# Two weight blocks loaded one step earlier, and two tiles of attention swapped, in a one-core masked attention kernel

## The chip, the cores and the metric

The kernel runs on one core of a Trainium2 chip. The metric is the device time of one execution in microseconds (us). The core's engines are TensorE (PE, with its weight loads as PEld), VectorE (DVE), ScalarE (ACT), GpSimd (POOL) and SyncE (SP). SP, ACT and POOL also issue transfers (DMAs), which run on the core's 16 DMA engines.

## The reference, cut to what matters

```python
h = jnp.maximum(_layernorm(x, axis=-1), 0.0)        # x: 2708 x 1024, float32
q = h @ W_q.T + b_q ; k = h @ W_k.T + b_k ; v = h @ W_v.T + b_v
z = (q @ k.T) / sqrt(1024)
z = z * adj ; z = jnp.where(z == 0.0, -10000.0, z)  # adj: 2708 x 2708 of 0 and 1, some 4 ones in a row
out = x + relu(softmax(z, axis=1) @ v)
```

`adj` is sparse, so a row of the attention has a handful of neighbours, and all other scores carry no weight. A row with no neighbour gets the mean over all rows.

## The kernel before, in words

**What is multiplied.** The kernel folds W_q and W_k into one matrix M, so that "q" means h @ M, and a score is the product of a q row with a neighbour's h row. W_v is applied behind attention, to the weighted sum of h rows. So there are two dense products, h @ M for the queries and u @ W_v for the outputs. Rows are sorted by their number of neighbours and cut into 21 tiles of 128 rows and a rest; tile t has K[t] slots for neighbours (tile 17 three, tile 13 five).

**Units.** Tiles go through TensorE in pairs ("units"): ten q pairs (units 0 to 9; the last, `last_q` = 9, holds tiles 18 and 19), then ten o pairs, (6, 5), (4, 3) and so on along the list `order`, and then the lone tile 8 (`alone`; its transposed rows are `T_alone`). A pair is multiplied by a seven-product scheme on 2 x 2 blocks. The blocks of the weight stand in `M[:, i, j]`, and combinations of them in `T[:, 0..3]`, which lies in the buffer `wlow`. The operands of a unit's own rows are `a11`, `a12`, `a22` and the sums `s1` to `s4`. One product is four matmuls of 128x512, eight records in the profile.

**The order of one unit.** `multiply(n)` makes five products, calls `between(n)`, which opens the next unit with its first two products (`opened(n + 1)`: a11 x M[0,0], and then s1 x T[:,0] for a q pair, s1 x M[0,1] for an o pair), and makes unit n's own last product, a22 x T[:,3]. Between the products `after(i)` puts in everything else: attention steps, loads of coming rows, and near the end of the q pairs the exchange of M for W_v.

**The exchange.** With B the blocks of W_v: B12 (less B11) goes to M[0,1] two units ahead. B22 is loaded into T[:,0], B11 into M[0,0], both at `after(0)` of the last q pair, and B21 into M[1,0] at its `after(3)`. VectorE then makes T[:,1], T[:,2] and T[:,3] from them by subtraction (the lines `nc.vector.tensor_sub(place, a, b)`), and ScalarE copies B22 on to M[1,1]. Two buffers in T[:,0] then serve attention's gathers. In the profile these loads are `wlow<-in_wv_dram` and `M<-in_wv_dram`.

**Attention** is a stream of VectorE steps that is fed into the units in portions (`advance`). For a tile: `fetch` loads its q rows (`pq`; from `q_late`, where the q pairs store them, for tiles from 8 on) and asks for the h rows of its neighbours (`g`, gathered by POOL into buffers as these come free); `scores` multiplies (line 863); `weights` forms the softmax; `sums` adds up u (line 923). u goes to `u_dram`, and the o pair's rows (`or`) come back from there.

**What sets the order.** In this part of the program VectorE keeps the order in which the code is written. The order on the other engines and queues is set by a scheduler ahead of time. Each engine and each queue works through its list in order.

Of the kernel before, what the change touches and what calls it, by code (L numbers as in the profile page):

```python
# [65 lines left out]
def tile_preln_masked_attention(  # L66
# [12 lines left out]
    nc = tc.nc  # L79
# [120 lines left out]
    M = core.tile([P, 2, 2, 4, NB], FT, name="M")  # L200
# [108 lines left out]
    def follow(steps):  # L309

        for step in steps.split():
            first, *only = step[1:].split(".")
            first, *last = first.split("-")
            first = int(first or 0)
            if step[0] == "s":
                stats(range(first, int(last[0] if last else first) + 1))
            elif step[0] == "m":
                moments(first)
            elif step[0] == "r":
                root(first)  # L320
            elif step[0] == "a":
                apply(first, *[range(int(o[0]), int(o[-1]) + 1) for o in only])
            elif step[0] in "hk":
                keep(first, step[0] == "h")
            elif step[0] == "+":
                owe(first)
            elif step[0] == "p":
                counted(first)
            elif step[0] == "c":
                counts(*halves[first])  # L330
            elif step[0] == "o":
                sorted_at.append(sort(*halves[first]))
            elif step[0] == "w":
                pooled.close()
                with tc.issue_after((behind if first < EARLY else products)[-1].ins):
                    entered.append(put(first, int(last[0]) + 1))
            elif step == "z":
                pooled.enter_context(tc.manual_schedule(engines={mybir.EngineType.Pool}))
                with tc.issue_after(entered[-1].ins):
                    reload(EARLY, NT)  # L340
            elif step[0] == "b":
                reload(*halves[first])
            elif step[0] == "g":
                squared(first)
            else:
                if step[0] == "e":
                    counted(first)
                if step[0] != "j":
                    found(first, *[range(int(o[0]), int(o[-1]) + 1) for o in only])
                if step[0] != "i":  # L350
                    listed(first)
# [81 lines left out]
    T = wlow.rearrange("p (k a) (b w) -> p k (a b) w", a=2, b=2)  # L433
# [12 lines left out]
    with tc.tile_pool(name="w", bufs=1, side="left") as wp:  # L446
# [11 lines left out]
        t1 = [work.tile([P, D], FT, tag="hT", name=f"t1_{k}", bufs=2) for k in range(2)]  # L458
# [145 lines left out]
    def small(name):  # L604
        return half.tile([P, NB], FT, tag="half", name=name, bufs=14)
# [380 lines left out]
    done, held, ws, us = set(), {}, {}, {}  # L986
    formed = set()
    faced_tiles, whole_second = set(), []
    order = [6, 5, 4, 3, 2, 0, 20, 7, 17, 13, 18, 12, 19, 11, 15, 10, 14, 1, 16, 9, 8]
    assert sorted(order) == list(range(FULL))  # L990
    chain = placed
    stream = attention(order[:order.index(0)] + [SECOND] + order[order.index(0):])
# [15 lines left out]
    def add_block(bank, a, b, last=True):  # L1008
        for c in range(4):
            mm = nc.tensor.matmul(bank, a[:, c, :], b[:, c, :], start=False, stop=(c == 3), skip_group_check=True)  # L1010
        return mm
# [3 lines left out]
    def opened(n):  # L1015

        if n not in banks_of:
            return
        X, Z = banks_of[n]
        ops = ops_of[n][0]  # L1020
        add_block(X, ops["a11"], M[:, 0, 0])
        Y = psum.tile([P, NB], FT, tag="acc", name="psy")
        nc.scalar.copy(Y, X)
        if n == FIRST:
            follow("o0")
        products.append(add_block(Z, ops["s1"], T[:, 0] if units[n][0] == "q" else M[:, 0, 1]))
        p5 = small("p5")
        nc.scalar.copy(p5, Z)
        opened_of[n] = Y, p5

    def between(n):

        if n == len(units) - 1:
            single["first"] = one_started(single["banks"], single["turned"][:, 0:4, :])
        else:
            opened(n + 1)

    def one_started(banks, a):

        X, Z = banks  # L1040
        add_block(X, a, M[:, 0, 0])
        first = small("p_single")
        nc.scalar.copy(first, X)
        return first

    def multiply(n, results, after):


        X, Z = banks_of.pop(n)
        ops = ops_of.pop(n)[0]  # L1050
        Y, p5 = opened_of.pop(n)
        after(0)
        after(1)
        products.append(add_block(Y, ops["s2"], T[:, 1]))
        u2 = small("u2")
        nc.scalar.copy(u2, Y)
        after(2)
        add_block(X, ops["a12"], M[:, 1, 0])
        results[0](X)
        after(3)  # L1060
        products.append(add_block(Z, ops["s4"], M[:, 1, 1]))
        results[2](Z, u2)
        after(4)
        products.append(add_block(Y, ops["s3"], T[:, 2]))
        results[1](Y, p5)
        after(5)
        between(n)
        add_block(Y, ops["a22"], T[:, 3])
        results[3](Y)
        after(6)  # L1070
# [119 lines left out]
    def of_wv(i, j):  # L1190

        return wv[j][:, i * 4:(i + 1) * 4, :]
# [26 lines left out]
    last_q = len(q_pairs) - 1  # L1219
# [13 lines left out]
    for n, unit in enumerate(units):  # L1233
# [15 lines left out]
        def after(i):  # L1249
# [15 lines left out]
                    with tc.issue_after(sorted_at[-1].ins):  # L1265
                        nc.vector.memset(g, 0.0)
            b11, t1, b21, b22 = M[:, 0, 0], M[:, 0, 1], M[:, 1, 0], M[:, 1, 1]
            for at, place, src in (((-2, 0), t1, of_wv(0, 0)), ((0, 0), T[:, 0], of_wv(1, 1)), ((0, 0), b11, of_wv(0, 0)),
                                   ((0, 3), b21, of_wv(1, 0))):
                if (n - last_q, i) == at:  # L1270
                    nc.sync.dma_start(place, src)
            if (n - last_q, i) == (0, 4):
# [302 lines left out]
```

## Time and profile before

| | us |
|---|---|
| median of 3 timed runs | 630.40 |
| lowest and highest | 630.32, 631.99 |
| the profiled execution | 635.63 |
| its span, first to last instruction | 633.9 |
| TensorE busy | 623.0 (98%) |
| VectorE busy | 525.2 (83%) |
| GpSimd busy | 370.7 (58%) |
| ScalarE busy | 291.6 (46%) |

All times inside the profile count from the span's start. A row of a timeline reads: start, duration, engine, line, operation, output<-inputs, count; in brackets the idle time of that engine ahead of it and what ended it. The mean granted clock of TensorE over the span is 0.994 of full speed.

### The profile page before, as it was taken

To read this page: it belongs to the slowest core of one execution; us is meant where nothing else is said; L and a number is where in the kernel's file an instruction comes from. 1 tells how busy PE (TensorE), PEld (TensorE's weight loads), DVE (VectorE), ACT (ScalarE), POOL (GpSimd) and SP (SyncE) were. 2 spreads that over 40 slices of the span, in tenths; PEclk is the share of its full clock that TensorE was granted. 3 is DMA by queue.
4 is the path that set the end of the run, shared out by engine and by line. 5 is a ranking of instruction groups with operands and counts; after the bars stand their busy time and mean duration, and the time that the engine had idled before them with its cause. 6 is when DMAs were issued, how large, how long until landed. Compare 5 with 4: busy or idle time off the path is not lost.

```text
span 633.9 us, 6066 instructions
## 1 busy us (share of the span) xinstructions
PE 623.0 (98%) x1579; PEld 312.0 (49%) x1579; DVE 525.2 (83%) x1022; ACT 291.6 (46%) x421; POOL 370.7 (58%) x394
## 2 busy tenths in 40 slices
PE   9999999999998999999999989999999999999996
PEld 5777766444444544444444434444444444444442
DVE  5999879898897845899897879998988998988741
ACT  3538985749477372443332333444433324342300
POOL 2639960885766677666543432878566776762241
PEclk9999999999999999999999989999999999999999
DMA  8999997598788469996686999899999999996391
GB/s 333 407 365 316 340 351 301 207 320 307 262 257 337 135 196 369 296 410 191 207 343 197 362 346 305 261 335 318 330 285 344 291 297 307 341 286 172 102 295 71
DMA packets 65089, 182.19 MB, mean 287 GB/s; under 512 B 9960, under 2 KB 20024, under 8 KB 64409
## 3 DMA queue, kind: packets, MB, share of 16 engines
q0 software_dynamic: 26656, 86.02, 43.3%
q1 hardware_dynamic: 31594, 71.53, 32.7%
q10 hardware_dynamic: 6798, 24.20, 9.8%
q8 instruction: 14, 0.23, 0.2%
q14 instruction: 27, 0.21, 0.1%
HBM read 146.70 MB, written 43.36 MB: 300 GB/s over the span
## 4 chain that ended last, share of the span: by engine, by line
PE 96%; DMA 3%; issue 0%; POOL 0%; SPq 0%; DVE 0%; ACT 0%; POOLq 0%
PE ps L1010 44%; PE psy L1010 32%; PE ps_y L476 6%; PE ps_x L476 4%; PE ps_z L476 4%; PE pt L415 3%; DMA M<-in_wv_dram 2%; DMA qr<-h_dram,tab 1%; PE ps_y L511 1%; PE ps_h L1226 0%; PE ps_v L594 0%; DVE y_alone L1391 0%; POOL out_dram L1375 0%; ACT q L1101 0%; POOLq L1397 0%
## 5 line engine op out<-in xcount | busy, mean ns | idle before, releaser
L610 POOL DMA_INDIRECT g<-h_dram,tab x93 | 120.5, 1296 | 62.7 <-ACT u L912 21.7
L1010 PE MATMUL ps<-M,a 128*128 128x512 f32 x320 | 145.8, 599 | 2.0 <-DMA M<-in_wv_dram 2.0
L1010 PE MATMUL psy<-wlow,s 128*128 128x512 f32 x320 | 145.1, 596 | 0.0
L863 DVE SCALAR_TENSOR_TENSOR junk<-g,pq 128x1024 uint8<-128x1024 f32 x92 | 112.4, 1221 | 11.8 <-issue 4.9
L1010 PE MATMUL ps<-M,s 128*128 128x512 f32 x240 | 107.9, 592 | 0.0
L1010 PEld LDWEIGHTS ps<-M,a 128*128 128x128 f32 x320 | 60.4, 192 | 75.4 <-issue 71.2
L1010 PEld LDWEIGHTS psy<-wlow,s 128*128 128x128 f32 x320 | 60.6, 192 | 72.9 <-issue 71.9
L923 DVE SCALAR_TENSOR_TENSOR u<-g,coef,u 128x1024 f32<-128x1024 f32 x70 | 89.7, 1281 | 5.5 <-ACT u L912 4.0
L389 DVE FIND_INDEX8 at<-ones,adj 128x8 uint32<-128x685 f32 (+1 forms) x88 | 74.5, 865 | 0.0
L1010 PEld LDWEIGHTS ps<-M,s 128*128 128x128 f32 x240 | 45.5, 190 | 57.2 <-issue 56.5
L1010 PE MATMUL psy<-wlow,a 128*128 128x512 f32 x160 | 71.9, 592 | 0.0
L368 ACT ACTIVATE sized<-adj 128x2708 uint8<-128x2708 f32 (+1 forms) x22 | 54.2, 2465 | 7.9 <-DMA adj<-in_adj_dram 6.6
L1111 POOL DMA_INDIRECT y<-in_x_dram,tab x19 | 34.6, 1821 | 35.6 <-ACT y L1128 24.2
L298 POOL TENSOR_TENSOR hsum<-hsum,x 128x256 f32<-128x256 f32 (+1 forms) x56 | 38.8, 738 | 25.5 <-DVE wlow L444 21.4
L1010 PEld LDWEIGHTS psy<-wlow,a 128*128 128x128 f32 x160 | 30.4, 190 | 38.3 <-issue 37.1
L808 POOL DMA_INDIRECT out_dram<-y,tab x21 | 27.0, 1287 | 19.2 <-issue 13.1
L1010 PE MATMUL ps<-wlow,s 128*128 128x512 f32 x80 | 36.0, 593 | 0.0
L944 ACT COPY v<-u 128x1024 f32<-128x1024 f32 x19 | 19.8, 1044 | 29.1 <-DVE u L923 25.8
L760 ACT COPY ps<-bp_sb 128x512 f32<-128x512 f32 x42 | 24.6, 595 | 10.3 <-DVE y L1146 9.7
L626 POOL DMA_INDIRECT tab_dram<-tab,pos_i x22 | 21.7, 985 | 11.2 <-DVE pos_i L689 5.7
L276 ACT ACTIVATE x<-x,r 128x1024 f32<-128x1024 f32 (+1 forms) x22 | 25.8, 1232 | 5.2 <-POOL r L266 5.2
L912 ACT ACTIVATE u<-g,coef 128x1024 f32<-128x1024 f32 x16 | 18.4, 1149 | 21.3 <-DVE coef L911 13.2
(253 smaller groups left out, 843.4 us busy)
## 6 DMA issues: line engine op xcount, KB each, us to landing
adj<-in_adj_dram SPq DMA_DIRECT2D x21, 1354.0 KB
x<-in_x_dram SPq DMA_DIRECT2D x21, 512.0 KB
h_dram<-x ACTq DMA_DIRECT2D x21, 512.0 KB
u_dram<-v ACTq DMA_DIRECT2D x19, 512.0 KB
or<-u_dram SPq DMA_DIRECT2D x76, 128.0 KB
q_late<-q SPq DMA_DIRECT2D x12, 512.0 KB
pq<-q_late POOLq DMA_DIRECT2D x12, 512.0 KB
M<-in_wv_dram SPq DMA_DIRECT2D x3, 1024.0 KB
```

Source lines behind the costliest of these rows:

```text
L276: nc.scalar.activation(xs[i][:n], xs[i][:n], AF.Relu, bias=r[:n, 4, i:i + 1], scale=r[:n, 3, i:i + 1])
L298: small.append(nc.gpsimd.tensor_add(hsum[:n, cols], hsum[:n, cols], xt[:n, cols]))
L368: nc.scalar.activation(sized[:n], a[:n, :, :PW], AF.Abs, accum_out=total[:n, t:t + 1])
L389: nc.vector.max_index(at[:n, k - first_k, g, :], ones[:n, 0:8], a[:n, g, :])
L476: mm = nc.tensor.matmul(bank, a_tile(o + H * a[0], a[1], i), b(o), start=first and o == 0, stop=(o == H - 1), skip_group_check=True)
L610: return nc.gpsimd.indirect_dma_start(out=dst, out_offset=None, in_=src, in_offset=off, bounds_check=N - 1, oob_is_err=False)
L760: nc.scalar.copy(return_[h], row[:, h * NB:(h + 1) * NB])
L808: to = nc.gpsimd.indirect_dma_start(out=out, out_offset=bass.IndirectOffsetOnAxis(ap=ptab.bitcast(U32)[:n, t, SLOTS:SLOTS + 1], axis=0), i ...
L863: chained(lambda: nc.vector.scalar_tensor_tensor(junk, g_of[t][s], 1.0, tq[t], op0=ALU.mult, op1=ALU.mult, accum_out=zall[:, t, s:s + 1]))
L923: chained(lambda: nc.vector.scalar_tensor_tensor(u, g_of[t][s], coef[:, s:s + 1], u, op0=ALU.mult, op1=ALU.add))
L1010: mm = nc.tensor.matmul(bank, a[:, c, :], b[:, c, :], start=False, stop=(c == 3), skip_group_check=True)
L1111: return nc.gpsimd.indirect_dma_start(out=y[:n], out_offset=None, in_=x, in_offset=off, compute_op=ALU.add)
```

## The change

It issues the loads of B22 and B11 directly behind the two products that open the last q pair, in `between` of the unit before, instead of at `after(0)` of the last q pair. And it swaps tiles 17 and 13 in `order`, so that attention takes 13 first; the o pair of the two is (13, 17) then.

```diff
-    order = [6, 5, 4, 3, 2, 0, 20, 7, 17, 13, 18, 12, 19, 11, 15, 10, 14, 1, 16, 9, 8]
+    order = [6, 5, 4, 3, 2, 0, 20, 7, 13, 17, 18, 12, 19, 11, 15, 10, 14, 1, 16, 9, 8]
...
         else:
             opened(n + 1)
+        if n == last_q - 1:
+            nc.sync.dma_start(T[:, 0], of_wv(1, 1))
+            nc.sync.dma_start(M[:, 0, 0], of_wv(0, 0))
...
-            for at, place, src in (((-2, 0), t1, of_wv(0, 0)), ((0, 0), T[:, 0], of_wv(1, 1)), ((0, 0), b11, of_wv(0, 0)),
-                                   ((0, 3), b21, of_wv(1, 0))):
+            for at, place, src in (((-2, 0), t1, of_wv(0, 0)), ((0, 3), b21, of_wv(1, 0))):
                 if (n - last_q, i) == at:
                     nc.sync.dma_start(place, src)
```

SyncE's queue around the loads, before and then now. `q_late<-q_2152` and `q_late<-q_2153` are the stores of q tiles 16 and 17 (the unit before the last q pair), and `or` are rows of o pairs.

```order
L1086 DMA q_late<-q_2152 128x1024
L700 DMA or_2258<-u_dram 32x4x256 x4
L700 DMA or_2263<-u_dram 32x4x256 x4
L1086 DMA q_late<-q_2153 128x1024
L1271 DMA wlow<-in_wv_dram 128x2048
L1271 DMA M<-in_wv_dram 128x2048 x2
L700 DMA or_2370<-u_dram 32x4x256 x4
```

```order
L1089 DMA q_late<-q_2152 128x1024
L700 DMA or_2258<-u_dram 32x4x256 x4
L700 DMA or_2263<-u_dram 32x4x256 x4
L1038 DMA wlow<-in_wv_dram 128x2048
L1039 DMA M<-in_wv_dram 128x2048
L1089 DMA q_late<-q_2153 128x1024
L1273 DMA M<-in_wv_dram 128x2048
```

The loads of B22 and B11 moved ahead of the store of q tile 17; the load of B21 stays behind it.

POOL's queue in the same stretch, before and then now, where `pq` is a load of a tile's q rows and `g` a gather of one neighbour slot. Before, `pq_2353` belongs to tile 17 and `pq_2434` to tile 13; now `pq_2353` belongs to tile 13 and `pq_2447` to tile 17.

```order
L845 DMA g_1428<-v_dram 64x1024
L610 DMA g_1430<-h_dram,tab 128x1024
L610 DMA g_1431<-h_dram,tab 128x1024
L610 DMA g_1432<-h_dram,tab 128x1024
L610 DMA g_1433<-h_dram,tab 128x1024
L610 DMA g_1434<-h_dram,tab 128x1024
L610 DMA g_1435<-h_dram,tab 128x1024
L610 DMA g_1425<-h_dram,tab 128x1024
L610 DMA g_1426<-h_dram,tab 128x1024
L610 DMA g_1428<-h_dram,tab 128x1024
L833 DMA pq_2353<-q_late 128x1024
L833 DMA pq_2434<-q_late 128x1024
```

```order
L845 DMA g_1428<-v_dram 64x1024
L833 DMA pq_2353<-q_late 128x1024
L610 DMA g_1430<-h_dram,tab 128x1024
L610 DMA g_1431<-h_dram,tab 128x1024
L610 DMA g_1432<-h_dram,tab 128x1024
L610 DMA g_1433<-h_dram,tab 128x1024
L610 DMA g_1434<-h_dram,tab 128x1024
L610 DMA g_1435<-h_dram,tab 128x1024
L610 DMA g_1425<-h_dram,tab 128x1024
L610 DMA g_1426<-h_dram,tab 128x1024
L610 DMA g_1428<-h_dram,tab 128x1024
L833 DMA pq_2447<-q_late 128x1024
```

The first load of q rows moved from behind the nine gathers to ahead of them; the second stays behind them.

## The prediction

> **What bounds the kernel now.** I read the page's busy times first, then its chain, then the chain in order of time, and last the instructions of each engine around the one place where the chain leaves TensorE near the edit.
>
> ```profile
> PE 623.0 (98%) x1579; PEld 312.0 (49%) x1579; DVE 525.2 (83%) x1022; ACT 291.6 (46%) x421; POOL 370.7 (58%) x394
> PE 96%; DMA 3%; issue 0%; POOL 0%; SPq 0%; DVE 0%; ACT 0%; POOLq 0%
> 197.56 5.28 DMA qr<-h_dram,tab
> 352.95 13.84 DMA M<-in_wv_dram
> 366.93 8.80 PE ps L1010 x16
> ```
>
> TensorE is busy 98% of the span and is 96% of the chain. So time can be won only where TensorE stands still or runs slowly. The chain leaves it for a transfer at two places: at 197.56 (a gather of rows for a q pair, which the change does not touch) and at 352.95, the load into M that the change issues earlier. Here is TensorE at both:
>
> ```profile
> 197.30 3.60 PE L1010 MATMUL ps<-M,s 128*128 128x512 f32 x8
> 202.98 1.54 PE L415 MATMUL pt<-ident,qr 128*128 128x128 f32 x8 [2.08 <-DMA qr<-h_dram,tab]
> 204.32 4.85 PE L1010 MATMUL psy<-wlow,s 128*128 128x512 f32 x8
> ...
> 344.13 3.60 PE L1010 MATMUL ps<-wlow,s 128*128 128x512 f32 x8
> 361.30 3.60 PE L1010 MATMUL psy<-wlow,s 128*128 128x512 f32 x8
> 366.93 5.37 PE L1010 MATMUL ps<-M,a 128*128 128x512 f32 x8 [2.03 <-DMA M<-in_wv_dram]
> 372.13 3.60 PE L1010 MATMUL ps<-M,s 128*128 128x512 f32 x8
> 375.57 3.60 PE L1010 MATMUL psy<-wlow,a 128*128 128x512 f32 x8
> ...
> 366.90:370.70 3.80, 3.77 (x5) 1.64 (x6) 1.36 (x2) 0.00 (x0) 2.86 (x3) 0.55 1.00 365
> ```
>
> One product is eight matmul records. Two products in a row start 375.57 - 372.13 = 3.44 us apart. The product at 361.30 (the last q pair) should be followed at 364.74 by the first product of the first output pair, which reads B11 from M[0,0]. It starts at 366.93: 2.19 us late. It then takes 372.13 - 366.93 = 5.20 us instead of 3.44, another 1.76 us. The window row (busy times of five engines, then the granted clock, the DMA share and GB/s) gives the reason: a clock of 0.55 in these 3.8 us. The same pair, an idle time of 2.08 us and a product of 4.85 us instead of 3.60, stands at 202.98. **What the wait for B11 costs in this execution is 2.19 + 1.76 = 3.95 us.**
>
> **The change, part by part.** *The two loads issue earlier.* SyncE's queue before:
>
> ```profile
> 338.67 4.46 SPq L700 DMA_DIRECT2D or<-u_dram  x8
> 351.81 0.34 SPq L1086 DMA_DIRECT2D q_late<-q  x1
> 352.25 0.38 SPq L1271 DMA_DIRECT2D wlow<-in_wv_dram  x1
> 352.95 5.44 SPq L1271 DMA_DIRECT2D M<-in_wv_dram  x2
> 358.49 16.24 SPq L700 DMA_DIRECT2D or<-u_dram  x8
> ```
>
> B22 (into T[:,0], "wlow") goes out at 352.25 and B11 at 352.95, because both stand behind the store of q tile 17 at 351.81, which waits for its eviction. Behind the edit they stand ahead of that store, and what they wait for is the last reader of their places: a11 x M[0,0], and then s1 x T[:,0], the product at 344.13, which ends at 347.73. So B22 can issue at about 347.8 and B11 0.7 us later, at 348.5, which is 4.45 us earlier. SyncE issued nothing between 343.1 and 351.8, so the wait at the head of its queue delays nothing there. The loads themselves cost no engine time; the count of loads stays the same.
>
> When does B11 land? The chain gives 13.84 us from issue to landing. With that, 348.5 + 13.84 = 362.3, which is 2.4 us before the 364.74 at which TensorE wants it. That it need not take longer, although nine gathers are in flight then, I bound by the traffic:
>
> ```profile
> 343.00:347.70 4.70, 4.70 (x13) 2.07 (x12) 4.59 (x5) 0.57 (x1) 3.79 (x4) 1.00 0.86 197
> 347.70:352.20 4.50, 4.50 (x12) 1.96 (x11) 4.43 (x5) 1.55 (x3) 3.55 (x4) 1.00 0.90 292
> 352.20:355.00 2.80, 2.80 (x8) 1.28 (x7) 2.80 (x5) 1.25 (x2) 2.00 (x2) 1.00 0.85 256
> 355.00:359.00 4.00, 4.00 (x11) 1.76 (x10) 3.40 (x14) 2.73 (x6) 0.73 (x1) 1.00 1.02 419
> ```
>
> From 355 on, the engines moved 419 GB/s; from 347.7 to 355 they moved 292 and 256. If the loads get nothing but that gap, they move (419 - 292) x 4.5 + (419 - 256) x 2.8 = 1.0 MB of their 2.1 MB by 355, half of what before began only then and ended at 366.8. The other half takes about half of those 11.8 us: 361. So both workings put B11 at 361 to 362.5, and the wait goes. Lower end, if they were alone at 419 GB/s: 5 us, about 353. Upper end: a duration over 16.2 us, which keeps a part of the wait.
>
> *The store of q tile 17* now stands behind 2.1 MB in the same queue. Its reader is the load of that tile's q rows ("pq"), on POOL's queue:
>
> ```profile
> 341.85 1.96 POOL L610 DMA_INDIRECT g<-h_dram,tab  x1 [7.75 <-ACT u L912]
> 353.99 1.74 POOL L610 DMA_INDIRECT g<-h_dram,tab  x1 [0.53 <-DVE u L929]
> 359.75 1.15 POOL L833 DMA_DIRECT2D pq<-q_late  x2 [4.02 <-DMA q_late<-q]
> 367.23 1.35 POOL L610 DMA_INDIRECT wlow<-h_dram,tab  x1 [6.33 <-DVE wlow L1282]
> ...
> 338.07 1.22 DVE L863 SCALAR_TENSOR_TENSOR junk<-g,pq 128x1024 uint8<-128x1024 f32 x1
> 364.17 2.29 DVE L1282 TENSOR_TENSOR wlow<-wlow,M 128x2048 f32<-128x2048 f32 x1 [1.71 <-DMA wlow<-in_wv_dram]
> 371.21 1.23 DVE L863 SCALAR_TENSOR_TENSOR junk<-g,pq 128x1024 uint8<-128x1024 f32 x1 [2.95 <-DMA pq<-q_late]
> 399.27 1.24 DVE L863 SCALAR_TENSOR_TENSOR junk<-g,pq 128x1024 uint8<-128x1024 f32 x1
> ```
>
> The store can start moving only when B11 has landed, so it lands at about 362 to 364, and POOL issues pq of tile 17 then, 2 to 4 us later than 359.75. Queued behind it on POOL are gathers into the two buffers made from T, which waited until 367.23 for VectorE's subtraction anyway, and which VectorE first uses at 399.27. Cost: nothing, with some 30 us of cover.
>
> *Tile 13 ahead of tile 17.* Its q rows were stored long before, and its pq buffer is free once the score at 338.07 is done. POOL was idle until 341.85, so this pq issues at about 339.4 and delays no gather. VectorE's wait of 2.95 us at 371.21 for tile 17's pq goes. So does its wait of 1.71 us for B22. That brings VectorE forward by 4.66 us, more than TensorE's 3.95. Both tiles keep their three and five gathers, and the gathers for both are issued by 354. No arithmetic is added.
>
> *Does the gain reach the end?* VectorE must keep up with a TensorE that is 3.95 us earlier, and the last tile must be ready:
>
> ```profile
> DVE p L1123 <- ACT taken L1077: 3.9, 4, 1.6
> DVE u L1127 <- PE ps L1010: 3.6, 5, 1.2
> 534.58 0.69 DVE L1127 TENSOR_TENSOR u<-ps,u 128x512 f32<-128x512 f32 x1 [0.57 <-PE ps L1010]
> ...
> 607.35 3.60 PE L1010 MATMUL psy<-wlow,s 128*128 128x512 f32 x8
> 609.07 1.25 DVE L705 STREAM_TRANSPOSE T_alone<-or 128x1024 f32<-128x1024 f32 x1 [10.76 <-DMA or<-u_dram]
> 610.78 3.60 PE L1010 MATMUL ps<-M,T_alone 128*128 128x512 f32 x8
> ```
>
> The two rows of waits are of the time behind 368: VectorE there stands 7.5 us in all for products and their evictions, the last such time at 534.58. So it is led by TensorE up to there and moves with it. The lone tile's transpose ends at 610.32, and its first product starts at 610.78, when 607.35 + 3.43 lets it: TensorE did not wait, but the spare time is only 0.46 us. As the work ahead of that transpose follows TensorE until 534.58, I let it move along. The cost is nothing, or some tenths.
>
> **Sum.** Against the profiled execution's own 635.63 us (span 633.9): 635.63 - 3.95 = 631.7. The median of the timed runs is 630.40, 5.2 us under the profiled one, and even under its span. TensorE runs at its full pace in the profile, so the timed runs must stand still less, or end sooner. Two losses of clock, 1.76 us here and about as much at 202.98, would be 3.5 of these 5.2 us, and the runs (630.32 to 631.99) differ by 1.67, about one such loss. So the gain in a timed run lies between 2.19 us (idle time alone) and 3.95 (with the slow product). The profile has the slow product behind both waits, the gap speaks for its absence; I take the middle, 3.1 us: 630.4 - 3.1 = **627.3 us**.
>
> On this the Trainium skill ("TensorE: Matmul & The Clock Gate", Part 1) says that the clock is halved after an idle window of about 3.4 us that runs freely, and takes a busy one to come back. The trace agrees with the length of the slow time but not with the idle time, which was 2.03 us here; by that rule alone the wait would cost its 2.19 us and the time would be 628.2. The skill's "Runtime: NRT & Kernel Launch" puts a fixed gap of about 6.2 us between a profile's total and the reported time. By that the timed runs hold the whole 3.95 us and the time would be 626.4; no run shown here can tell.
>
> **The rivals.** *B11 still late.* The loads share the queues with nine gathers; if they need over 16.2 us, a wait stays, and with it perhaps the slow clock. For it: 0.90 share of DMA at 347.7. Against: 292 GB/s there, where 419 were possible. Time: 629 to 630.4. *The gain is given back at the end.* The lone tile has 0.46 us to spare; if attention moves along only in part, TensorE waits 1 to 3 us ahead of that product instead: 629.5 to 631.5. Against: the row at 534.58. *Slower: the last tile comes later than now.* Attention's fetches are reordered for all later tiles, through buffers that come free in another order. On the old time axis the lone tile is wanted at 610.78 - 3.95 = 606.8. If its transpose ended at 610.9, 0.6 us later than now, TensorE would wait 4.1 us there and, with a slow product behind it (1.76), lose 5.9 us for the 3.95 won: 632.3 or more. That is the point from which it decides. Against: VectorE's 7.5 us of waiting behind 368 absorb that much delay. *Nothing to win in timed runs:* their loads are faster than the profiled one's, and the wait is 1 us or less: 629.5 to 630.4.
>
> **How the numbers follow.** The wait goes and the time follows: 0.62, with 625.8 to 628.5. Wait gone but under 1 us in timed runs: 0.12. B11 still late: 0.08. Given back at the end: 0.08. Slower: 0.10. About 0.3%, 1.9 us, is what a measurement of this kernel can tell from no change. So faster 0.62, within 0.28, slower 0.10. The range reaches from 625.8 (the full 3.95 and some tenths) to 630.6 (no gain), and leaves the slower case out.
>
> **What would show it.** In the changed profile: B22 and B11 issued at about 348; no idle time of TensorE for M near 365 and a clock of 1.0 there; products 3.44 us apart from 197 us' wait to the end; no wait for pq near 367 on VectorE; the store of tile 17 landing at 362 to 364; T_alone at 605 to 606. The prediction is wrong if TensorE stands still elsewhere for as long, above all ahead of T_alone, or if the timed runs had no such wait.

## The result: 627.9 us, 0.5% faster

| | before | changed |
|---|---|---|
| median of 5 timed runs, us | 631.17 | 627.91 |
| lowest and highest, us | 630.32, 631.99 | 627.52, 628.29 |
| the profiled execution, us | 635.63 | 628.18 |
| its span, us | 633.9 | 626.5 |

The ratio is 0.9953, with a 95% interval of 0.9942 to 0.9965; by the medians that is 3.26 us. (The ratios are those of fast runs as the record gives them, and can differ a little from the quotient of two medians.) The prediction was 627.3 us. The profiled execution of the changed kernel is one of its five timed runs; that of the kernel before is not among its five.

The page of the changed kernel, busy times and then the shares of the chain:

```profile
PE 619.6 (99%) x1579; PEld 310.9 (50%) x1579; DVE 525.1 (84%) x1022; ACT 291.1 (46%) x421; POOL 366.2 (58%) x394
PE 99%; POOL 0%; DVE 0%; POOLq 0%; issue 0%
```

The chain now never leaves TensorE for a transfer. Both transfers are gone from it, the load of B11 and also the gather near 197 that the change does not touch. TensorE at both places (start, duration, engine, line, what):

```profile
201.13 1.04 PE L415 MATMUL pt<-ident,qr 128*128 128x128 f32 x8
357.73 3.60 PE L1010 MATMUL psy<-wlow,s 128*128 128x512 f32 x8
361.16 3.60 PE L1010 MATMUL ps<-M,a 128*128 128x512 f32 x8
364.60 3.60 PE L1010 MATMUL ps<-M,s 128*128 128x512 f32 x8
```

The first product with B11 follows at 357.73 + 3.43 = 361.16, without idle time, and lasts 3.60 us instead of 5.37. Times here stand some 3.6 us ahead of those of before, because the wait near 197 did not happen in this execution. The queues and VectorE around the loads:

```profile
344.19 0.35 SPq L1038 DMA_DIRECT2D wlow<-in_wv_dram  x1
344.59 0.43 SPq L1039 DMA_DIRECT2D M<-in_wv_dram  x1
348.24 0.33 SPq L1089 DMA_DIRECT2D q_late<-q  x1
...
359.88 0.57 POOL L833 DMA_DIRECT2D pq<-q_late  x1 [7.74 <-DMA q_late<-q]
...
362.80 1.22 DVE L863 SCALAR_TENSOR_TENSOR junk<-g,pq 128x1024 uint8<-128x1024 f32 x1
```

The loads go out 4.05 and 3.65 us ahead of the store of q tile 17. That store lands when POOL issues the load behind it, at 359.88. VectorE's next scores, at 362.80, are those of tile 13 and wait for nothing. The traffic in the second and third of the four windows that the prediction showed, moved by the 3.6 us to the axis of this execution:

```profile
344.10:348.60 4.50, 4.50 (x12) 1.99 (x11) 4.43 (x5) 1.52 (x3) 3.57 (x4) 1.00 1.01 386
348.60:351.40 2.80, 2.80 (x8) 1.25 (x7) 2.80 (x5) 1.28 (x2) 1.98 (x2) 1.00 1.01 408
```

The loads filled most of the gap: 386 and 408 GB/s, where before there were 292 and 256. No row prints when B11 landed, but the trace holds the completion events of its load, and the last of them stands at 356.79. That is 12.2 us behind the issue and 4.4 us before TensorE wants B11.

### The profile page after: what moved, and what is told of

Same layout as the page of the kernel before. It is cut to its first block, busy times and chain, and to the rows that moved or that the text cites. A ratio compares the mean times of both kernels' runs of the same rounds, so it can differ in the third digit from the quotient of the medians.

```text
span 626.5 us, 6070 instructions
## 1 busy us (share of the span) xinstructions
PE 619.6 (99%) x1579; PEld 310.9 (50%) x1579; DVE 525.1 (84%) x1022; ACT 291.1 (46%) x421; POOL 366.2 (58%) x394
## 4 chain that ended last, share of the span: by engine, by line
PE 99%; POOL 0%; DVE 0%; POOLq 0%; issue 0%
PE ps L1010 46%; PE psy L1010 33%; PE ps_y L476 7%; PE ps_x L476 4%; PE ps_z L476 4%; PE pt L415 3%; PE ps_y L511 1%; PE ps_h L1229 0%; PE ps_v L594 0%; DVE y_alone L1393 0%; POOL out_dram L1377 0%; POOLq L1399 0%; POOL hsum L121 0%; PE ps_in L678 0%; PE ps_all L680 0%
## 5 line engine op out<-in xcount | busy, mean ns | idle before, releaser
L610 POOL DMA_INDIRECT g<-h_dram,tab x92 | 114.0, 1239 | 58.9 <-DVE u L923 18.5
L1010 PE MATMUL ps<-M,a 128*128 128x512 f32 x320 | 144.0, 593 | 0.0
L863 DVE SCALAR_TENSOR_TENSOR junk<-g,pq 128x1024 uint8<-128x1024 f32 x91 | 111.1, 1221 | 7.3 <-DMA g<-h_dram,tab 3.1
L923 DVE SCALAR_TENSOR_TENSOR u<-g,coef,u 128x1024 f32<-128x1024 f32 x68 | 87.1, 1281 | 3.9 <-ACT u L912 2.4
L626 POOL DMA_INDIRECT tab_dram<-tab,pos_i x22 | 21.6, 982 | 14.7 <-DVE pos_i L689 9.2
```

Source lines behind the costliest of these rows:

```text
L610: return nc.gpsimd.indirect_dma_start(out=dst, out_offset=None, in_=src, in_offset=off, bounds_check=N - 1, oob_is_err=False)
L863: chained(lambda: nc.vector.scalar_tensor_tensor(junk, g_of[t][s], 1.0, tq[t], op0=ALU.mult, op1=ALU.mult, accum_out=zall[:, t, s:s + 1]))
L923: chained(lambda: nc.vector.scalar_tensor_tensor(u, g_of[t][s], coef[:, s:s + 1], u, op0=ALU.mult, op1=ALU.add))
```

## Experiments

The kernels ran in three sets, each on a chip of its own, beside runs of the kernel before on the same chip. Those had medians of 633.4 us (29 runs), 633.8 (30) and 634.2 (18). Only ratios within a set are compared.

**The kernel before, again** (first set; no edit).

> The kernel before, unchanged, profiled once more. Theory (two kinds of wait): the wait for B11 is in every execution, and the wait at 197 us (a gather for a q pair) is a chance of the first profile, which is why that profile's 635.63 us lie over every timed run. Then the new profile is 630 to 632 us in total, has no wait at 197, and has TensorE late by about 2.2 us ahead of the first product that reads B11, with or without a slow product behind it (1.76 us). Rival (the profiler lengthens things): the new profile is again near 635 us with both waits. Timed: 630.3 to 632 by either.

Measured: 633.67 us (631.07 to 636.32), ratio 0.9992 (0.9974 to 1.0010). The profiled execution took 636.32. TensorE in it:

```profile
203.65 1.08 PE L415 MATMUL pt<-ident,qr 128*128 128x128 f32 x8 [2.52 <-DMA qr<-h_dram,tab]
204.56 5.29 PE L1010 MATMUL psy<-wlow,s 128*128 128x512 f32 x8
...
367.50 5.37 PE L1010 MATMUL ps<-M,a 128*128 128x512 f32 x8 [1.92 <-DMA M<-in_wv_dram]
```

Both waits stand there with a slow product behind each. That run is only the longest of a wide spread: of the 29 runs of before beside it, the longest took 636.2 without a profile. So a run can be as long without a profile (and the profiled execution of the third set, 629.69 us, is among the shortest of its twelve); executions differ in which waits they have. My expectation that the wait near 197 was a chance of the first profile fails on this chip, and so does the time, 630.3 to 632.

**The changed kernel, again** (second and third set; no edit).

> The changed kernel once more, profiled and timed on the chip of this set. Theory: the change takes away the one wait for B11, so it is faster than the kernel before by 2.2 us (idle time) to 4 us (with the slow product), whatever else a chip adds. The wait at 197 us stands ahead of everything the change moves; if it is here, both kernels have it and the times of both are higher. Rival (the first result's gain came in part from the wait at 197 being absent): no gain over 1 us here.

> The changed kernel again, beside the one with the store in another queue on the same chip. Theory: 3 us (2.2 to 4) under the kernel before, no wait of TensorE near 361 to 378; a wait at 197 may be there.

Measured: 630.72 us (629.48 to 631.69), ratio 0.9947 (0.9926 to 0.9968); and 630.40 (629.54 to 633.14), ratio 0.9951 (0.9931 to 0.9971). By the medians the gain is 3.06 and 3.78 us. TensorE and VectorE in the second set's profile:

```profile
202.96 1.58 PE L415 MATMUL pt<-ident,qr 128*128 128x128 f32 x8 [2.11 <-DMA qr<-h_dram,tab]
204.34 4.81 PE L1010 MATMUL psy<-wlow,s 128*128 128x512 f32 x8
...
368.14 3.60 PE L1010 MATMUL ps<-M,s 128*128 128x512 f32 x8
368.76 0.69 DVE L1096 TENSOR_TENSOR q<-psy,p 128x512 f32<-128x512 f32 x1
371.58 3.60 PE L1010 MATMUL psy<-wlow,a 128*128 128x512 f32 x8
...
604.67 1.25 DVE L705 STREAM_TRANSPOSE T_alone<-or 128x1024 f32<-128x1024 f32 x1 [10.21 <-DMA or<-u_dram]
606.80 3.60 PE L1010 MATMUL ps<-M,T_alone 128*128 128x512 f32 x8
```

This is the best pair with the profile of before, since both have the wait near 197 with its slow product, and so one time axis. The second product of the first output pair starts at 368.14 instead of 372.13, 3.99 us earlier. The lone tile's first product starts at 606.80 instead of 610.78, 3.98 us earlier. Nothing of the gain is lost in the 239 us between. The third set's profile has the wait near 197, but no slow product:

```profile
202.55 1.06 PE L415 MATMUL pt<-ident,qr 128*128 128x128 f32 x8 [1.89 <-DMA qr<-h_dram,tab]
203.45 3.60 PE L1010 MATMUL psy<-wlow,s 128*128 128x512 f32 x8
```

**The early loads without the swap** (first set). The edit to the changed kernel:

```diff
-    order = [6, 5, 4, 3, 2, 0, 20, 7, 13, 17, 18, ...
+    order = [6, 5, 4, 3, 2, 0, 20, 7, 17, 13, 18, ...
```

> The early loads of B22 and B11, with tile 17 still ahead of tile 13. Theory: the loads carry the whole gain, since only they touch what TensorE waits for: 627.9 us, within 0.6 of the changed kernel, no wait of TensorE near 361. The store of q tile 17 lands behind the loads, so VectorE waits for tile 17's q rows 3 to 6 us instead of 2.95, and makes it good later, where it waits for products anyway. Rival: that wait pushes VectorE so far back that evictions come late and TensorE stands still: 629 to 631 us.

Measured: 638.63 us (636.25 to 640.02), ratio 1.0074 (1.0051 to 1.0098), slower than before. My theory fails here; the rival named what happens, but 629 to 631 us for it. TensorE, two pieces of the chain, and VectorE:

```profile
364.91 3.60 PE L1010 MATMUL ps<-M,a 128*128 128x512 f32 x8
377.54 5.72 PE L1010 MATMUL psy<-wlow,a 128*128 128x512 f32 x8 [5.61 <-DVE q L1096]
...
351.99 12.65 DMA q_late<-q
365.16 9.20 DMA pq<-q_late
...
374.38 1.23 DVE L863 SCALAR_TENSOR_TENSOR junk<-g,pq 128x1024 uint8<-128x1024 f32 x1 [7.74 <-DMA pq<-q_late]
```

The wait for B11 is gone, yet two products later TensorE stands still for 5.61 us, and the product behind that is slow (5.72). It waits for VectorE's line 1096, an eviction that has to read this product's bank before the product adds to it. VectorE works in the order of the code, and ahead of that eviction stand tile 17's scores. These wait 7.74 us for its q rows, which are stored (12.65 us) and loaded again (9.20) while the transfer engines are full (a DMA share of 0.99 to 1.13 from 352 to 374.4). In the repeated changed kernel above, with tile 13 in this place, the eviction starts at 368.76 and ends 2.1 us before its product.

**The same, with the store of tile 17 on another queue** (third set). The edit to the kernel without the swap:

```diff
-            (nc.scalar if t < 4 else nc.sync).dma_start(dst, q)
+            (nc.scalar if t < 4 or t == 17 else nc.sync).dma_start(dst, q)
```

> The loads early and tile 17 still ahead of 13, as in the kernel with the loads only, but the store of q tile 17 goes out on ScalarE's queue, so that it does not stand behind the two loads. Theory (two costs of the loads without the swap): the store's place behind the loads made that kernel some 5 us slower than before; with the store in another queue most of that goes. But VectorE still waits for tile 17's q rows ahead of the eviction that frees the bank of TensorE's third next product (22.0 us apart from nothing: before the change that eviction ended only 1.3 us ahead of its product, and TensorE now comes 4 us sooner), so TensorE waits 1 to 3 us there, and the time lies within 1.5 us of the kernel before, and 2 us or more over the changed kernel. Rival 1 (only the store's place costs): as fast as the changed kernel. Rival 2 (the store lands late for want of bandwidth, whatever its queue): as slow as with the loads only, 4 us or more over the kernel before.

(The words "apart from nothing" in it are a slip and mean nothing.) Measured: 638.17 us (637.60 to 639.44), ratio 1.0062 (1.0039 to 1.0084). The chain, and TensorE's row:

```profile
351.97 9.13 DMA q_late<-q
361.63 12.42 DMA pq<-q_late
...
377.23 5.29 PE L1010 MATMUL psy<-wlow,a 128*128 128x512 f32 x8 [5.32 <-DVE q L1096]
```

The store is 3.5 us quicker on ScalarE's queue, and the load behind it is 3.2 us slower. The two together take 9.13 + 12.42 = 21.6 us, against 12.65 + 9.20 = 21.9. So the place in SyncE's queue is not what makes tile 17 late, and the theory fails. The second rival's time came out (4.0 us over the kernel before, by the medians): with the engines as full as above (a share of 0.98 to 1.06), tile 17's rows arrive 22 us behind the issue of their store by either queue. Before the change, with the weight loads behind that store, it was 371.21 - 351.81 = 19.4 us. That the early megabytes push the others back is the reading that fits all three; the bytes of each transfer were not counted.

**The swap without the early loads** (first set). The edit to the changed kernel puts the loads back at `after(0)`:

```diff
-        if n == last_q - 1:
-            nc.sync.dma_start(T[:, 0], of_wv(1, 1))
-            nc.sync.dma_start(M[:, 0, 0], of_wv(0, 0))
...
-            for at, place, src in (((-2, 0), t1, of_wv(0, 0)), ((0, 3), b21, of_wv(1, 0))):
+            for at, place, src in (((-2, 0), t1, of_wv(0, 0)), ((0, 0), T[:, 0], of_wv(1, 1)), ((0, 0), b11, of_wv(0, 0)),
+                                   ((0, 3), b21, of_wv(1, 0))):
```

> The swap of tiles 13 and 17, with the loads where they were. Theory: TensorE still waits for B11, so 630 to 631.5 us; VectorE no longer waits for q rows of tile 17. Rival: the load of one tile's q rows (0.5 MB) leaves the crowded time from 355 on, so B11 lands up to 1.2 us earlier and the swap alone brings up to 1.2 us of idle time, and the slow product too if it hangs on the length of the idle time: 628 to 630 us.

Measured: 632.66 us (630.82 to 636.07), ratio 0.9998 (0.9977 to 1.0020). TensorE:

```profile
202.64 1.06 PE L415 MATMUL pt<-ident,qr 128*128 128x128 f32 x8 [1.80 <-DMA qr<-h_dram,tab]
203.54 3.60 PE L1010 MATMUL psy<-wlow,s 128*128 128x512 f32 x8
...
360.49 3.60 PE L1010 MATMUL psy<-wlow,s 128*128 128x512 f32 x8
366.05 3.67 PE L1010 MATMUL ps<-M,a 128*128 128x512 f32 x8 [1.96 <-DVE q L1096]
```

The product with B11 still starts at 366.05 instead of 360.49 + 3.43 = 363.92, 2.13 us late. The profile puts this idle time down to VectorE, but it was the load. The last completion event of B11's load stands at 365.91 in this trace, 14.04 us behind its issue at 351.87 and 0.14 us ahead of the product, the same 0.14 us as before the change (366.79 and 366.93). And the product does not need the eviction that the row names: before the change it starts at 366.93, while that eviction starts only at 367.58, and in the second set at 364.71, ahead of that eviction's start at 365.75. The swap alone gains nothing.

**The loads later still** (first set). To the kernel with the swap alone, a wait that holds both loads until the first product of the last q pair is done:

```diff
-            for at, place, src in (... ((0, 0), T[:, 0], of_wv(1, 1)), ((0, 0), b11, of_wv(0, 0)), ...
+            for at, place, src in (... ((0, 2), T[:, 0], of_wv(1, 1)), ((0, 2), b11, of_wv(0, 0)), ...
                 if (n - last_q, i) == at:
-                    nc.sync.dma_start(place, src)
+                    load = nc.sync.dma_start(place, src)
+                    if at == (0, 2):
+                        tc.add_manual_dep(load.ins, products[-1].ins.name, ...)
```

> The swap, and both loads held until the first product of the last q pair is done, some 2.5 us later than before the change. Theory (every us by which B11 is late goes to the end): idle time of TensorE ahead of B11's product of 4 to 5 us with a slow product behind it, and 633 to 635 us. Rival (attention or the lone tile is the true bound, and TensorE's wait is partly hidden): under 632 us.

Measured: 634.30 us (631.92 to 640.25), ratio 1.0016 (0.9990 to 1.0041). TensorE, and the issue of the first load:

```profile
202.87 1.69 PE L415 MATMUL pt<-ident,qr 128*128 128x128 f32 x8 [2.30 <-DMA qr<-h_dram,tab]
204.35 4.70 PE L1010 MATMUL psy<-wlow,s 128*128 128x512 f32 x8
...
354.50 0.35 SPq L1271 DMA_DIRECT2D wlow<-in_wv_dram  x1
361.18 3.60 PE L1010 MATMUL psy<-wlow,s 128*128 128x512 f32 x8
368.40 6.35 PE L1010 MATMUL ps<-M,a 128*128 128x512 f32 x8 [3.63 <-DMA M<-in_wv_dram]
374.59 3.60 PE L1010 MATMUL ps<-M,s 128*128 128x512 f32 x8
```

With the load issued 2.4 us later (352.25 before, the axis shifted by 0.1), the product comes 368.40 - 364.61 = 3.79 us late, and takes 374.59 - 368.40 = 6.19 us instead of 3.44. That is 6.5 us lost at this place instead of 3.95. The 634.30 us lie in the range of the theory, but so would they with no effect at all, as the kernel before takes 633.4 on this chip. In the timed runs only 1.6 us more than the swap alone are seen, and the interval includes no difference to before: less than the theory asked for, with the right sign.

**One of the two loads early** (second set). To the changed kernel, first B11 goes back to `after(0)` (only B22 early), then B22 does (only B11 early):

```diff
             nc.sync.dma_start(T[:, 0], of_wv(1, 1))
-            nc.sync.dma_start(M[:, 0, 0], of_wv(0, 0))
...
+            ... ((0, 0), b11, of_wv(0, 0)), ...
```
```diff
-            nc.sync.dma_start(T[:, 0], of_wv(1, 1))
             nc.sync.dma_start(M[:, 0, 0], of_wv(0, 0))
...
+            ... ((0, 0), T[:, 0], of_wv(1, 1)), ...
```

> Swap, and only B22 loaded early; B11 stays behind the store of tile 17. Theory (the loads share one queue and one amount of traffic): B22's megabyte is out of the way when B11 starts, so B11 lands 2 to 4 us earlier than before the change and TensorE's wait is gone or under 0.5 us: within 1 us of the changed kernel. Rival (B11's own issue time sets its landing): the wait stays near 2 us, and the time at that of the kernel before.

> Swap, and only B11 loaded early; B22 stays behind the store of tile 17. Theory: no wait for B11, and B22 lands by about 362 to 364 us, before VectorE's subtraction delays anything that TensorE reads (its first reader on TensorE comes two products after B11's): within 0.5 us of the changed kernel. Rival: the subtraction, late and in VectorE's fixed order, pushes the evictions back and TensorE waits there: 1 us or more slower than the changed kernel.

Measured: 631.63 us (629.17 to 632.83), ratio 0.9957 (0.9939 to 0.9975) with B22 alone early; 631.47 (629.77 to 635.22), ratio 0.9968 (0.9947 to 0.9990) with B11 alone. TensorE with B22 alone early:

```profile
202.97 1.06 PE L415 MATMUL pt<-ident,qr 128*128 128x128 f32 x8 [1.96 <-DMA qr<-h_dram,tab]
203.87 5.29 PE L1010 MATMUL psy<-wlow,s 128*128 128x512 f32 x8
...
364.72 3.60 PE L1010 MATMUL ps<-M,a 128*128 128x512 f32 x8
```

and with B11 alone early:

```profile
203.42 1.06 PE L415 MATMUL pt<-ident,qr 128*128 128x128 f32 x8 [2.13 <-DMA qr<-h_dram,tab]
204.32 3.60 PE L1010 MATMUL psy<-wlow,s 128*128 128x512 f32 x8
...
363.48 3.60 PE L1010 MATMUL ps<-M,a 128*128 128x512 f32 x8
```

Neither profile has a wait for B11. It suffices to take one megabyte out of its way: with B22 gone ahead, B11 issues at 352.19, only 0.76 us earlier than before on the same axis, and its last completion event stands at 362.35, 10.2 us later instead of 13.84. Both ratios agree with that of the whole change within their intervals. By the medians B11 alone is 0.75 us slower than it, between what the theory (0.5) and the rival (1) said, so these runs leave that open.

**The other wait** (second set). The rows of h gathered near 197 are stored by ScalarE when it has normalised them. The edit takes that step for one group of tiles (a8, k8) ahead of ScalarE's pass over one tile's adjacency rows (p17):

```diff
-                (2, 2): "p16", (2, 3): "p17 a8 k8 z", ...
+                (2, 2): "p16", (2, 3): "a8 k8 p17 z", ...
```

> The changed kernel, with ScalarE's normalisation and storing of h tiles 8 to 10 put ahead of one pass over adj (2.46 us each) in the third q pair. Theory: the wait at 197 us is for the landing of these stores, so they land up to 2.5 us earlier and the wait goes or shrinks to below 0.5 us: where the changed kernel has that wait, 2 to 4 us faster than it, else the same. Rival: that pass over adj, now later, holds up VectorE's search or a buffer's next load and the time is the same or worse.

Measured: 632.91 us (630.21 to 636.51), ratio 0.9989 (0.9966 to 1.0013) against before: slower than the changed kernel. TensorE, and VectorE's row near it:

```profile
200.73 1.04 PE L415 MATMUL pt<-ident,qr 128*128 128x128 f32 x8
202.74 0.09 DVE L389 MATCH_VALUE_LOAD at<-ones,adj 128x8 f32 x1 [4.91 <-DMA adj<-in_adj_dram]
211.35 0.24 PE L678 MATMUL ps_in<-sort,before 128*128 128x144 bf16 x1 [1.83 <-DVE sort L666]
212.68 5.40 PE L1010 MATMUL ps<-wlow,s 128*128 128x512 f32 x8 [1.03 <-DVE s L722]
```

The wait for the gather is absent (no idle time at 200.73), but so it was in the first profile of the changed kernel, so this one profile does not show that the edit removed it. The pass that was put back holds the next load of adjacency rows. VectorE waits 4.91 us for these, and some 9 us later TensorE waits for VectorE twice and has its slow product after all. No version here beats the change.

## Why the prediction was right, and where it was not

**The wait and its price.** Right. All three profiles of the changed kernel lack the wait for B11, and 3.98 us reach the end on a common axis, for the predicted 3.95.

**The gap between the profiled execution and the timed runs.** The time came out right, but this step failed. I read the 5.2 us as slow products that timed runs lack. By the sums below, what lacked was a whole wait. What TensorE loses at the two places (idle time, and what the records there exceed 1.04 and 3.60 us by) accounts for the time of each profiled execution above that of the changed kernel, 628.18:

| profiled execution | lost near 197 | lost at B11 | sum | time above 628.18 |
|---|---|---|---|---|
| changed, third set | 1.9 | 0 | 1.9 | 1.5 |
| B11 alone early | 2.1 | 0 | 2.1 | 2.3 |
| B22 alone early | 3.7 | 0 | 3.7 | 3.7 |
| changed, second set | 3.9 | 0 | 3.9 | 3.5 |
| before | 3.8 | 3.8 | 7.6 | 7.5 |
| before, again | 4.3 | 3.7 | 7.9 | 8.1 |
| loads later still | 4.1 | 6.4 | 10.4 | 10.2 |

(Third set: 1.89 and nothing; before: 2.08 + 0.50 + 1.25, and 2.03 + 1.77.) They agree within 0.4 us. (The other four have losses at other places too, and with these they agree within 0.5 us: 4.9 against 5.3 for the swap alone, 11.4 against 11.8 and 11.1 against 10.8 for the two kernels without the swap, 4.7 against 4.6 for the sooner store of h.) By this sum, timed runs of before at 630.32 to 631.99 us, on a chip where the changed kernel's are at 627.5 to 628.3, would have no loss near 197 and 2.2 to 3.95 us at B11: some with the slow product, some without. That is inferred from the times, not seen in rows. If so, the middle that I took, 3.1 us, came near the 3.26 measured for another reason than mine, and that nearness is in part luck.

On the Trainium skill's fixed gap of about 6.2 us between a profile's total and the reported time ("Runtime: NRT & Kernel Launch", "The ~15µs preamble/postamble breakdown"): no such gap shows here between a profiled execution and the others, as the changed kernel's profiled 628.18 us lies among its timed runs of 627.52 to 628.29. Both 635.63 and 628.18 are reported times, 1.7 us above their own spans, so a gap between a total and a reported time cannot lie between them; the total that the page speaks of is in no run here.

**The landing of B11.** Mis-sized a little, to the safe side: by the completion events 12.2 us from issue to landing (11.84 and 12.35 in the second and third set) instead of the 13.84 that I carried over, so 4.4 us to spare instead of 2.4. The traffic was near what I let the loads have up to 419 GB/s: (386 - 292) x 4.5 + (408 - 256) x 2.8 = 0.85 MB more than before in the two stretches, for the 1.0 MB of the prediction. The experiment with one load early shows how little was needed.

**The store of tile 17, "cost: nothing, with some 30 us of cover".** It landed where it was said (359.88 here, 363.4 on the axis of before), and in the change it costs nothing. But the working named only POOL's gathers as what stands behind it. It did not ask what VectorE has queued behind the scores of the tile that comes first. That is the eviction for the third product ahead. In the profile of before it stands on VectorE, as line 1093, at

```profile
373.63 0.69 DVE L1093 TENSOR_TENSOR q<-psy,p 128x512 f32<-128x512 f32 x1
```

and its product starts at 375.57: 1.25 us to spare, with TensorE 3.95 us late. Without that lateness the product is due at 371.62, ahead of the eviction's start. So with tile 17 first, 2.70 us up to the eviction's end at 374.32 would be lost even with its q rows as early as before; the rest comes from their arriving later. With tile 17 first and its store behind the loads, the measured cost is 5.61 us of idle time and a slow product, more than the loads gain.

**The swap.** Under-rated: I counted it as 2.95 us of VectorE's time brought forward. The runs show that the early loads need it. Alone, the loads give 1.0074 and the swap 0.9998; together they give 0.9947 to 0.9953.

**The end.** Right. VectorE and attention moved along, as the row at 534.58 had let expect; in the second set the lone tile's rows were ready at 604.67 + 1.25 = 605.92, within the 605 to 606 forecast, and TensorE did not wait for them.

**The rivals.** B11 still late, gain given back at the end, and slower by the lone tile did not happen. "Nothing to win in timed runs" is excluded by three intervals, all below 0.9972.

## What to carry to other kernels

Before a wait of the bounding engine is removed, look at the engine that evicts for it: what stands in its order between its present step and the eviction that the bounding engine will now want earlier, and does one of those steps wait for a transfer? Bytes that are moved earlier through busy engines can make other bytes late, even from another queue, so put a consumer that does not need those bytes first. And before a wait in one profiled execution is priced, add up all such waits and compare with the spread of the timed runs: some of them come and go from run to run and from chip to chip.

## What the runs showed of the hardware

An idle time of TensorE near 2 us can halve the clock behind it, or not (a granted clock of 0.51 from 368.90 to 370.70 in the profile of before). A product of 4.25 to 5.37 us instead of 3.60 came behind idle times of 1.92, 1.94, 1.96, 2.03, 2.08, 2.11, 2.30, 2.52 and 2.57 us. None came behind 1.80, 1.89, 1.96 and 2.13 us. Behind 3.63 us the product took 6.35. The length of the idle time does not decide it between 1.92 and 2.13 us; what does was not tested. The Trainium skill ("TensorE: Matmul & The Clock Gate", Part 1) asks for an idle window of about 3.4 us; these runs show the slow clock after much less.

A store of 0.5 MB and the load of the same bytes took 21.9 and 21.6 us together while the engines were full (a DMA share of 0.98 to 1.13), with the store on SyncE's queue and on ScalarE's: what the store gained, 3.5 us, the load lost but for 0.3.
